# A four-layer graph network on one core: read-outs moved between a block's scores and its products, and a new order for the end of layers two and three

## The chip, the core and the metric

The kernel runs on one core of one Trainium2 chip. The time is the device time of one execution in microseconds (us); several executions are taken and their median is given. The profile records one execution. Its times count from the start of the recorded span. Engines are called as the profile calls them: PE (matrix products), DVE (vector work), ACT (activations, copies), POOL (here it issues the gathers), SP (here it issues the plain transfers to and from memory).

## What is computed

The input is `x`, 4096 rows of 256 floats, and a 4096 x 4096 adjacency matrix `adj` that is symmetric, has ones on its diagonal and otherwise about two ones in a thousand. Four layers of attention over each row's neighbours follow one another, each with a norm before and the input added behind:

```python
h = relu(layernorm(x)); x = x + _L0(h, adj, W, a)      # 4 heads, elu
h = relu(layernorm(x)); x = x + _L1(h, adj, W, a)      # 1 head
h = relu(layernorm(x)); x = x + _L2(adj, h, w, b, phi) # 4 heads
h = relu(layernorm(x)); x = x + _L3(h, adj, Wq, ...)   # q, k, v, 4 heads

def _L1(node, adj, W, a):
    h = node @ W
    e = leaky_relu((h @ a[:F, 0])[:, None] + (h @ a[F:, 0])[None, :], 0.01)
    att = softmax(where(adj > 0, e, NEG_INF), axis=1)
    return h + att @ node

def _L2(adj, input, weights, biases, phis):
    x_prime = einsum('nd,hdf->hnf', input, weights) + biases
    S = leaky_relu(s_src[:, :, None] + s_dst[:, None, :], 0.2)
    return concat_heads(softmax(where(mask, S, -1e9)) @ x_prime)

def _L3(x, edge, Wq, bq, Wk, bk, Wv, bv):
    q, k, v = heads(x @ Wq + bq), heads(x @ Wk + bk), heads(x @ Wv + bv)
    scores = q @ k.T / sqrt(64) + (edge.T - 1) * 10000
    return merge(softmax(scores) @ v)
```

## The kernel before

The code counts layers from 0, so the layers two and three of the title are `l == 1` and `l == 2`; below, "layer 1" and "layer 2" are the code's. The rows were sorted by their number of neighbours and cut into 32 blocks of 128 rows (one row per partition). Block 0 holds the rows with most neighbours (23 slots), block 31 those with fewest (3 slots).

A first part (`lists`, `scan`) reads the adjacency matrix into lists of neighbours; `late` finishes layer 0. Then `layer(1)`, `layer(2)` and `layer(3)` run, all by the function `layer` (L1349). Each layer reads a table in memory (`tab[l]`) with one row per node, and layers 1 and 2 write the table of the next one: while layer `l` runs over its blocks, the rows of layer `l+1` are made from the blocks that are finished.

`layer` is a loop of 32 steps over the blocks in the order `ORDER` = 0, 30, 1, 29, ... 14, 16, 15, 31: it alternates large and small blocks, and ends with 14, 16, 15, 31. In a step these parts come, each for the block that it is due for:

- `fill` (L1368): POOL issues one indirect gather per neighbour slot (`fetch`, L1048), up to `AHEAD` = 4 steps ahead, into a ring in on-chip memory. The first gather of a layer waits until all rows of its table are in memory.
- `scores` (L1538): for layer 2 DVE adds the two score parts (L1553, L1554), the leaky slope (L1565), the maximum (L1596) and subtracts it (L1597); ACT takes the exponential (L1600). For layer 1 ACT adds (L1550, L1551), DVE compares neighbour lists (L1608, L1612), takes slope and maximum (L1565, L1592), and ACT the exponential (L1594).
- `weigh` (L1615): DVE sums and inverts (L1626, L1627), scales the shares (L1628), the row's own part (L1639) and the gathered rows (L1654, up to eight slots at a time, two at a time in the last two blocks); PE adds all slots up in PSUM by products with the identity (L1634, L1662), and a last product (L1668) ends the block.
- `settle` (L1675): DVE sums the two halves of PSUM into `x` (L1689) and takes the norm's statistics (L960, L962). The first half of `normed` is ACT's chain of eight small instructions (L965 to L972).
- `norm`: ACT makes `h` (L975), PE transposes it (L985, two instructions). `flip`: ACT copies the transpose out of PSUM as `ht` (L987).
- `product`: the first part of `advance` (L1695): PE multiplies `ht` with the next layer's weights (L1028). In layer 1 that is one product of width 264 (`we_l`); in layer 2 a product `wkv` of width 512 and a product `w_q` of width 256, which shares a PSUM bank with the next transposes where it can.
- `third`: the second part of `advance`. In layer 1 the row is copied out of PSUM by ACT (L1710), or for the last two blocks of ORDER by DVE with the bias added (L1708), and SP sends it to memory (L1712). In layer 2 DVE adds the bias to k and v into a tile `kv` (L1728), SP sends it (L1730), DVE adds the bias to q (L1732), multiplies q with k (L1735), reduces that per head into `eself` (L1739), and ACT takes the sums of squares of q and of k (L1742, two instructions with a read of the accumulator each).

`advance`, `settle` and `turned` are generators: each part of them runs where the loop calls `next`. Names: "norm 31" is the norm of block 31, "sum 16" the L1689 of block 16, "kv13" the L1728 of block 13, "ht14" the L987 of block 14, "squares 19" the two L1742 of block 19.

The order in which each engine executes is the order in which the code issues: an engine takes its instructions one after another, and one that waits holds up those behind it on the same engine. `upto(name, k)` runs a part for all blocks of ORDER up to place `k`. The loop sets how many steps each part trails: the sum by `S` (2, or 1 in the last five steps), the norm by `N` (3, then 2), the row's product by `Q` (5, 4, 3, 2 towards the end), its read-out by `T = Q + 1`.

Four PSUM banks are lent and given back by name (`bank`, `give`), so a product can wait for the read-out of an earlier one. The tiles `kv` come from a pool with three buffers (L1727): the L1728 of a block overwrites the tile of the block three earlier, once everything that reads that tile is done. The row's read-outs wait for the last product of an earlier step (`told_by`, `signals`) in place of their own product where that stands behind it on PE. At the end of layer 2 a check of the bounds (`verdict`, L1758) reads the squares.

The core of the old order in `layer`, cut:

```python
upto("norm", i - N); upto("product", i - Q)
p = self.scores(l, b, self.rows[b], g)
sums[b] = self.weigh(l, b, ..., g, p)
upto("settle", i - S); upto("flip", i - F); upto("third", i - T)
```

Of the kernel before, what the change touches and what calls it, by code (L numbers as in the profile page):

```python
# [20 lines left out]
D = 256  # L21
# [34 lines left out]
ORDER = [0, 30] + [b for k in range(1, 15) for b in (k, 30 - k)] + [15, 31]  # L56
# [24 lines left out]
class Sparse:  # L81
# [365 lines left out]
    def constants(self):  # L447
# [5 lines left out]
        for k, by in enumerate((MARK + PAIR, MARK)):  # L453
# [217 lines left out]
    def sort(self):  # L671
# [677 lines left out]
    def layer(self, l):  # L1349


        nc, nt, vs = self.nc, self.nt, {}
        wide = (W, WL, W, 2 * D)[l]
        slots = RING // wide
        ring = self.ring[:, : slots * wide].rearrange("p (k w) -> p k w", w=wide)
        todo, held, at = list(ORDER), {}, 0
# [67 lines left out]
        sums, behind, turning, flipped, rows = {}, {}, {}, {}, {}  # L1424
# [49 lines left out]
        def third(d):  # L1474
            if l < 3:
                step, wrote = when["row", d]
                self.reads = []
                next(rows.pop(d), None)
                if step < now:
                    for i in self.reads:  # L1480
                        told_by(i, wrote, step)
            while made and (len(made) > 1 or todo == []):
                i = self.send(*made.pop(0)).ins
                next_in_line(i)
                self.tc.declare_no_dep(i, group="results", reason="places differ")
                self.tc.add_to_no_dep_group("results", i)

        stages = {"settle": settle, "norm": norm, "flip": flip, "product": product, "third": third}
        done = {name: 0 for name in stages}

        def upto(name, k):
            while done[name] <= k:
                stages[name](ORDER[done[name]])
                done[name] += 1

        for i in range(nt):
            now = i
            left = nt - 1 - i
            if l == 3:
                S = 1 if left < 3 else 2  # L1500
                N = F = Q = S + 1
                T = N
            else:
                S = 1 if left < 5 else 2
                N = 2 if left < 4 else 3
                Q = 2 if left < 2 else 3 if left < 4 else 4 if left < 6 else 5
                F, T = max(N, Q - 1), Q + 1
            fill(i)
            if (l, i) == (2, 4):
                self.symmetric()  # L1510
            b = ORDER[i]
            upto("norm", i - N)
            upto("product", i - Q)
            g = ring[:, held[b][0] : held[b][1], :]
            p = self.scores(l, b, self.rows[b], g)
            if l == 3:
                upto("third", i - T)
            sums[b] = self.weigh(l, b, vs.pop(b) if l == 3 else self.rows[b][:, 0:D], g, p)
            start, end = held.pop(b)
            past.append((start * wide, end * wide, self.read))  # L1520
            self.ever.append((start * wide, end * wide, self.read[0]))
            if l < 3:
                signals[i] = self.read[1]
            upto("settle", i - S)
            if l < 3:
                upto("flip", i - F)
                upto("third", i - T)
        now = nt
        upto("norm", nt - 2)
        upto("third", nt - 3)  # L1530
        upto("product", nt - 2)
        upto("settle", nt - 1)
        upto("norm", nt - 1)
        upto("third", nt - 2)
        upto("product", nt - 1)
        upto("third", nt - 1)

    def scores(self, l, b, mine, g):  # L1538

        nc, pool = self.nc, self.pool  # L1540
        H = 1 if l == 1 else 4
        G = self.slots(l, b)
        K = CAPS[b]
        more = b == 0
        e = pool.tile([P, TOPK, H], F32, name=f"s_e_{l}_{b}", tag="e", bufs=3)
        ek = e[:, : K + 1, :].rearrange("p k h -> p (k h)")
        if l < 3:
            src = mine[:, D + H : D + 2 * H]
            if l == 1:
                nc.scalar.activation(e[:, :G, 0], g[:, :G, D], AF.Identity, bias=src)  # L1550
                nc.scalar.activation(e[:, K, :], mine[:, D : D + H], AF.Identity, bias=src)  # L1551
            else:
                first = nc.vector.tensor_tensor(e[:, K, :], mine[:, D : D + H], src, ALU.add)  # L1553
# [11 lines left out]
            steep = nc.vector.scalar_tensor_tensor(ek, ek, slope, ek, ALU.mult, ALU.max)  # L1565
# [34 lines left out]
        nc.scalar.activation(p[:, : K + 1, :].rearrange("p k h -> p (k h)"), ek, AF.Exp)  # L1600
        return p, p, None
# [13 lines left out]
    def weigh(self, l, b, me, g, made):  # L1615
# [6 lines left out]
        exps, p, tot = made  # L1622
# [20 lines left out]
        if more:  # L1643
            rows = self.more_rows(l, p, g[:, KEPT, :])
# [50 lines left out]
    def advance(self, l, b, ht, made):  # L1695
# [5 lines left out]
        if l == 2:  # L1701
# [5 lines left out]
            if short:  # L1707
                i = nc.vector.tensor_tensor(mine, ps, self.be2, ALU.add)  # L1708
            else:
                i = nc.scalar.copy(mine, ps)  # L1710
            self.reads.append(i.ins)
            nc.sync.dma_start(out=self.tab[2][ts(b, P), :], in_=mine)  # L1712
        else:
# [14 lines left out]
            i = nc.vector.tensor_tensor(kv, ps, self.bqkv[:, D:], ALU.add)  # L1728
# [52 lines left out]
class Net:  # L1781
# [341 lines left out]
    def dot_attention(self, wq, bq, wk, bk, wv, bv):  # L2123
        nc, tc, nt, n, nb = self.nc, self.tc, self.nt, self.n, self.nb
        scale = 1.0 / 8.0
        with ExitStack() as ctx:
# [88 lines left out]
            for b in range(nb):  # L2215
# [45 lines left out]
                while waiting:  # L2261
                    weigh()
# [58 lines left out]
```

## Time and profile before

| what | us |
|---|---|
| runs shown | 1676.06, 1674.33, 1669.05; median 1674.33 |
| the profiled execution | 1670.3 |
| its span, first to last instruction | 1668.5 |
| busy in the span: POOL, DVE, PE, ACT | 1142.3, 1108.8, 1074.4, 536.1 |

Cut at the first and last gathers of the layers, the same execution divides as follows (busy time of the engines in each stretch):

| stretch | us | PE | DVE | ACT | POOL |
|---|---|---|---|---|---|
| lists of neighbours | 0 to 375 | 248.8 | 271.2 | 204.4 | 229.1 |
| rest of layer 0 | 375 to 545 | 109.9 | 120.7 | 67.9 | 117.7 |
| layer 1, gathers | 545 to 875.9 | 232.5 | 163.0 | 110.4 | 250.2 |
| its end, no gathers | 875.9 to 902.7 | 16.4 | 10.6 | 10.7 | 0.95 |
| layer 2, gathers | 902.7 to 1240.2 | 238.8 | 215.1 | 104.5 | 255.6 |
| its end, no gathers | 1240.2 to 1275.2 | 25.5 | 22.3 | 16.1 | 0.95 |
| layer 3 | 1275.2 to 1668.5 | 202.5 | 305.9 | 22.3 | 287.8 |

In the lists of instructions by time, a line gives the start, the busy time, the engine, the source line, the operation with its output and inputs, the shape, and in brackets how long the engine had been idle before and what ended that; no bracket means that the engine went straight on. In the lines by stretches, each engine has its busy time and its number of instructions, and `PEclk` is the granted clock of PE as a share of full speed.

### The profile page before, as it was taken

How to read it: one execution, taken by the hardware profiler on the slowest of the kernel's cores; microseconds unless marked ns; L12 is line 12 of the kernel's file. 1: busy time of each engine (PE TensorE's matmuls, PEld its weight loads, DVE VectorE, ACT ScalarE, POOL GpSimd, SP SyncE). 2: the span in 40 equal slices, each digit the busy share in tenths (PEclk: the TensorE clock that was granted, in tenths of full speed). 3: DMA queues.
4: the chain of work that ended last, by engine and by line, in shares of the span. 5: the costliest groups of instructions: out<-in, count | busy, mean ns of one | idle time of the engine just before them, and what ended most of it. 6: DMA issues, size and time to landing. Idle time of an engine off the chain costs nothing.

```text
span 1668.5 us, 14028 instructions
## 1 busy us (share of the span) xinstructions
PE 1074.4 (64%) x3166; PEld 583.3 (35%) x3179; DVE 1108.8 (66%) x2651; ACT 536.1 (32%) x1754; POOL 1142.3 (68%) x1241
## 2 busy tenths in 40 slices
PE   5858888605775367787773567777793455546465
PEld 4513333203443234444442234444352232323232
DVE  5669899816885255555552456777774897888786
ACT  6966664103354033343342023333342000000000
POOL 1267777767774777777772777777753777777775
PEclk9969899857898678788897689999997677877777
DMA  7899999466552444444452445444543777767674
GB/s 267 298 395 394 365 394 331 147 222 162 155 166 69 119 120 127 132 131 134 131 137 65 108 111 148 133 139 133 142 123 106 210 220 205 213 206 211 201 209 132
DMA packets 125908, 309.07 MB, mean 185 GB/s; under 512 B 35028, under 2 KB 53463, under 8 KB 125816
## 3 DMA queue, kind: packets, MB, share of 16 engines
q0 software_dynamic: 66832, 203.64, 42.5%
q1 hardware_dynamic: 58984, 104.46, 17.8%
q8 instruction: 27, 0.44, 0.1%
q14 instruction: 65, 0.53, 0.1%
HBM read 273.00 MB, written 35.00 MB: 185 GB/s over the span
## 4 chain that ended last, share of the span: by engine, by line
POOL 25%; DVE 22%; DMA 20%; issue 15%; ACT 8%; PE 8%; DVEq 0%; POOLq 0%; ACTq 0%; SPq 0%
POOL s_ring L1048 20%; DMA s_ring<-s_tab,s_near 12%; DMA s_raw<-in_adj_dram 6%; DVE s_ring L1654 5%; POOL s_g L1048 2%; DMA s_g<-s_tab,s_keep 2%; POOL s_placed L722 2%; DVE s_ring L1575 1%; ACT s_low L277 1%; PE s_acc L1272 1%; PE s_acc L1662 1%; PE s_bank L1028 1%; DVE s_e L1579 1%; PE s_ps_t L1028 1%; POOL out_dram L1065 1%
## 5 line engine op out<-in xcount | busy, mean ns | idle before, releaser
L1048 POOL DMA_INDIRECT s_ring<-s_tab,s_near x900 | 855.9, 951 | 338.0 <-issue 264.8
L1662 PE MATMUL s_acc<-s_ring,s_ident 128*128 128x512 f32 (+1 forms) x1002 | 459.8, 616 | 275.6 <-DVE s_ring L1654 275.1
L1662 PEld LDWEIGHTS s_acc<-s_ring,s_ident 128*128 128x128 f32 x1002 | 222.2, 229 | 489.7 <-DVE s_ring L1654 305.2
L1048 POOL DMA_INDIRECT s_g<-s_tab,s_keep x192 | 182.8, 952 | 128.5 <-DMA s_raw<-in_adj_dram 66.1
L1654 DVE TENSOR_TENSOR s_ring<-s_ring,s_shares 128x2048 f32<-128x2048 f32 (+1 forms) x153 | 232.9, 1552 | 0.0
L277 ACT ACTIVATE s_low<-s_raw 128x1024 fp8e4<-128x1024 int32 x128 | 135.0, 1055 | 58.6 <-DMA s_raw<-in_adj_dram 56.8
L1600 ACT ACTIVATE s_shares<-s_e 128x40 f32<-128x40 f32 (+7 forms) x64 | 13.1, 205 | 332.7 <-DVE s_e L1597 332.7
L520 PE MATMUL s_pt<-s_low,s_mark_True 128*128 128x512 fp8e4 x256 | 83.9, 408 | 53.2 <-DVE s_cand L532 46.6
L1575 DVE TENSOR_TENSOR s_ring<-s_ring,s_shares 128x2048 f32<-128x2048 f32 (+7 forms) x47 | 78.8, 1676 | 56.4 <-DMA s_ring<-s_tab,s_near 36.4
L965 ACT ACTIVATE s_y<-s_mv,s_eps 128x1 f32<-128x1 f32 x64 | 18.8, 294 | 276.4 <-DVE s_mv L962 250.4
L532 DVE MAX8 s_cand<-s_pt 128x8 f32<-128x256 f32 x256 | 93.1, 416 | 13.8 <-PE s_pt L530 12.3
L1608 DVE TENSOR_SCALAR s_eq<-s_ring,s_own_f 128x207 bf16<-128x207 f32 (+12 forms) x32 | 12.6, 393 | 134.0 <-DMA s_ring<-s_tab,s_near 133.6
L631 PE MATMUL s_ae<-s_g,s_ident 128*128 128x512 f32 x192 | 93.0, 614 | 3.0 <-DVE s_g L622 2.9
L1579 DVE TENSOR_REDUCE s_e<-s_ring 128x32 f32<-128x2048 f32 (+7 forms) x47 | 78.9, 1679 | 1.6
L1028 PE MATMUL s_bank<-s_wkv,s_ht 128*128 128x512 f32 x128 | 63.6, 621 | 3.5 <-ACT s_ht L987 3.5
L520 PEld LDWEIGHTS <-s_mark_True 128*128 128x128 bf16 x256 | 23.6, 101 | 104.8 <-issue 61.1
L1634 PE MATMUL s_acc<-s_rx,s_ident 128*128 128x256 f32 x192 | 59.3, 392 | 0.0
L1028 PE MATMUL s_ps<-s_we_l,s_ht 128*128 128x264 f32 x128 | 43.7, 493 | 23.5 <-ACT s_ht L1310 23.5
L1668 PE MATMUL s_acc<-s_me,s_ident 128*128 128x256 f32 x192 | 57.6, 382 | 0.0
L1307 PE MATMUL s_pht<-s_ident,s_rx 128*128 128x128 f32 x64 | 14.0, 323 | 66.0 <-DMA s_ring<-s_tab,s_near 49.3
L622 DVE TENSOR_TENSOR s_g<-s_g,s_pe 128x1536 f32<-128x1536 f32 x32 | 55.4, 1735 | 0.0
L924 PE MATMUL s_bank<-s_to,s_to_row 128*128 128x32 f32 (+1 forms) x6 | 1.8, 393 | 81.8 <-DVE s_to L918 81.8
(286 smaller groups left out, 1830.8 us busy)
## 6 DMA issues: line engine op xcount, KB each, us to landing
s_raw<-in_adj_dram SPq DMA_DIRECT2D x128, 512.0 KB, 9.6
s_ring<-s_tab,s_near POOLq DMA_INDIRECT x900, 2.9
s_rx<-s_placed SPq DMA_DIRECT2D x32, 262.0 KB, 3.3
s_tab<-s_kv SPq DMA_DIRECT2D x32, 256.0 KB, 2.3
s_tab<-s_rx SPq DMA_DIRECT2D x32, 132.0 KB, 1.9
s_keep<-in_x_dram SPq DMA_DIRECT2D x8, 512.0 KB, 7.5
s_vself<-s_tab SPq DMA_DIRECT2D x32, 128.0 KB, 3.5
s_tab<-s_keep SPq DMA_DIRECT2D x7, 528.0 KB, 3.7
```

The costliest lines, as they stand in the source:

```text
L277: nc.scalar.activation(low[r][:, quarter(q)], raw.pop(q), AF.Copy, saturate=False, accum_out=self.sums[:, r, h : h + 1],)
L520: nc.tensor.matmul(pt, lhsT=self.mark[k], rhs=lo[:, k * PAIR + g * IB : k * PAIR + (g + 1) * IB], start=(k == 0), stop=False,)
L532: nc.vector.max(out=cand[:, g * (IB // CH) + k, :], in_=pt[:, ts(k, CH)])
L631: self.behind(got, nc.tensor.matmul(acc, lhsT=self.ident, rhs=g[:, :, k, 0:D], start=False, stop=(k == E - 1)))
L1028: self.writes(self.nc.tensor.matmul(ps[:, :width], lhsT=ht[:, c, :], rhs=w[:, c, :], start=(c == 0 and bias is None), stop=(c == KC - 1),))
L1048: return self.nc.gpsimd.indirect_dma_start(out=out, out_offset=None, in_=table[:, :], in_offset=bass.IndirectOffsetOnAxis(ap=idx, axis=0),)
L1575: scaled = nc.vector.tensor_tensor(kq, kq, q.unsqueeze(1).to_broadcast([P, m, D]), ALU.mult)
L1579: nc.vector.tensor_reduce(e[:, k0 : k0 + m, :], kq.rearrange("p k (h d) -> p k h d", h=4), AX.X, ALU.add)
L1634: self.took_x[b] = nc.tensor.matmul(acc[:, 1, :], lhsT=self.ident, rhs=self.x[b], start=True, stop=False)
L1654: scaled = nc.vector.tensor_tensor(v, v, p[:, k0 : k0 + m, :].unsqueeze(3).to_broadcast([P, m, H, D // H]), ALU.mult)
L1662: self.behind(self.got.get((l, b), ()), nc.tensor.matmul(acc[:, 0:n, :], lhsT=self.ident, rhs=g[:, k : k + n, v0 : v0 + D], start=False, s ...
L1668: last = nc.tensor.matmul(acc[:, 0, :], lhsT=self.ident, rhs=mev, start=False, stop=True).ins
```

## The change

The parts stay the same; the loop that orders them is written anew, and the second part of `advance` is cut in two in layer 2.

- Layers 1 and 2, all but the last two steps: `third` (the row's read-out and its transfer) runs between a step's `scores` and its `weigh`, where it ran behind the step's `settle` and `flip`.
- The last two steps of both layers: the last block's scores are issued directly behind the last but one block's products and norm; sum 16 goes ahead of block 15's products, and sum 15 ahead of block 31's.
- Layer 2: q times k, its reduction and the two squares become a part `rest` of their own. With more than four steps left it runs right behind `third`. After that it is left until `third` is about to run for the block three later (`upto("rest", done["third"] - 3)`), and at the end for all that remain. The kv pool keeps its three buffers.
- `self.turns`, which picks one of two buffers for the shares, is counted on in `scores` in place of `weigh`, as two blocks' scores can now be open.
- Layer 3 keeps its order.

```diff
-                next(rows.pop(d), None)
+                upto("rest", done["third"] - 3)
+                next(rows[d], None)
...
+        def rest(d):
+            next(rows.pop(d), None)
...
-        for i in range(nt):
-            now = i
-            left = nt - 1 - i
...
-            upto("norm", i - N)
-            upto("product", i - Q)
-            g = ring[:, held[b][0] : held[b][1], :]
-            p = self.scores(l, b, self.rows[b], g)
-            if l == 3:
-                upto("third", i - T)
-            sums[b] = self.weigh(l, b, vs.pop(b) if l == 3 else self.rows[b][:, 0:D], g, p)
...
-            upto("settle", i - S)
-            if l < 3:
-                upto("flip", i - F)
-                upto("third", i - T)
-        now = nt
-        upto("norm", nt - 2)
-        upto("third", nt - 3)
-        upto("product", nt - 2)
-        upto("settle", nt - 1)
-        upto("norm", nt - 1)
-        upto("third", nt - 2)
-        upto("product", nt - 1)
-        upto("third", nt - 1)
+        def score(i):
+            b = ORDER[i]
+            if i not in scored:
+                scored[i] = self.scores(l, b, self.rows[b], block(i))
+
+        def weigh(i):
...
+            sums[b] = self.weigh(l, b, me, block(i), scored.pop(i))
...
+        def shape(i):
+            upto("norm", i)
+            upto("flip", i)
+            upto("product", i)
+
+        for i in range(nt):
+            left = nt - 1 - i
...
+            elif left > 1:
+                S = 1 if left < 5 else 2
+                N = 2 if left < 4 else 3
+                Q = 3 if left < 4 else 4 if left < 6 else 5
+                upto("norm", i - N)
+                upto("product", i - Q)
+                score(i)
+                upto("third", i - Q - 1)
+                if left > 4:
+                    upto("rest", i - Q - 1)
+                weigh(i)
+                upto("settle", i - S)
+                upto("flip", i - max(N, Q - 1))
+            elif left == 1:
+                upto("norm", i - 2)
+                upto("product", i - 2)
+                score(i)
+                upto("settle", i - 1)
+                upto("third", i - 3)
+                weigh(i)
+                upto("norm", i - 1)
+                score(i + 1)
+            else:
+                shape(i - 2)
+                upto("third", i - 3)
+                upto("settle", i - 1)
+                weigh(i)
+                upto("third", i - 2)
+                shape(i - 1)
+                upto("settle", i)
+                upto("norm", i)
+                upto("third", i - 1)
+                shape(i)
+                upto("third", i)
+                upto("rest", i)
...
         p = self.shares[:, ts(self.turns % 2, TOPK * H)].rearrange("p (k h) -> p k h", h=H)
+        self.turns += 1
...
-        self.turns += 1
...
             self.reads.append(i.ins)
+            yield
             qk = pool.tile([P, 4, 64], F32, name=f"s_qk_{b}", tag="qk", bufs=2)
```

More of the change, by code (lines that the diff above doesn't have):

```diff
@@ L1486, in third @@
                 self.tc.add_to_no_dep_group("results", i)
-        stages = {"settle": settle, "norm": norm, "flip": flip, "product": product, "third": third}
+        def rest(d):
+            next(rows.pop(d), None)
+        stages = {
+            "settle": settle, "norm": norm, "flip": flip, "product": product, "third": third,
+            "rest": rest,
+        }
         done = {name: 0 for name in stages}
@@ L1494, in upto @@
                 done[name] += 1
-        for i in range(nt):
-            now = i
-            left = nt - 1 - i
-            if l == 3:
[L1500 to L1510, printed above, removed]
-            b = ORDER[i]
-            upto("norm", i - N)
-            upto("product", i - Q)
-            g = ring[:, held[b][0] : held[b][1], :]
-            p = self.scores(l, b, self.rows[b], g)
-            if l == 3:
-                upto("third", i - T)
-            sums[b] = self.weigh(l, b, vs.pop(b) if l == 3 else self.rows[b][:, 0:D], g, p)
+        block = lambda i: ring[:, held[ORDER[i]][0] : held[ORDER[i]][1], :]
+        scored = {}
+        now = 0
+        def score(i):
+            b = ORDER[i]
+            if i not in scored:
+                scored[i] = self.scores(l, b, self.rows[b], block(i))
+        def weigh(i):
+            nonlocal now
+            b = ORDER[i]
+            me = vs.pop(b) if l == 3 else self.rows[b][:, 0:D]
+            sums[b] = self.weigh(l, b, me, block(i), scored.pop(i))
             start, end = held.pop(b)
@@ L1522, in layer @@
             if l < 3:
-                signals[i] = self.read[1]
-            upto("settle", i - S)
-            if l < 3:
-                upto("flip", i - F)
-                upto("third", i - T)
-        now = nt
-        upto("norm", nt - 2)
-        upto("third", nt - 3)
-        upto("product", nt - 2)
-        upto("settle", nt - 1)
-        upto("norm", nt - 1)
-        upto("third", nt - 2)
-        upto("product", nt - 1)
-        upto("third", nt - 1)
+                signals[i], now = self.read[1], i + 1
+        def shape(i):
[4 more added lines that the diff above has]
+            left = nt - 1 - i
+            fill(i)
+            if (l, i) == (2, 4):
+                self.symmetric()
+            if l == 3:
+                S = 1 if left < 3 else 2
+                score(i)
+                upto("third", i - S - 1)
+                weigh(i)
[11 more added lines that the diff above has]
+                weigh(i)
+                upto("settle", i - S)
+                upto("flip", i - max(N, Q - 1))
+            elif left == 1:
+                upto("norm", i - 2)
+                upto("product", i - 2)
+                score(i)
+                upto("settle", i - 1)
[7 more added lines that the diff above has]
+                upto("settle", i - 1)
+                weigh(i)
+                upto("third", i - 2)
[6 more added lines that the diff above has]
+                upto("rest", i)
+        if l == 3:
+            upto("third", nt - 3)
+            upto("settle", nt - 1)
+            upto("third", nt - 1)
     def scores(self, l, b, mine, g):
```

## The prediction

> **What bounds the kernel now.** I read the granted clock and span first, then busy time by stretches, then the gathers on POOL, then the two tails on each engine in order of time.
>
> ```profile
> core 0: us, PE busy (x) PEld busy (x) DVE busy (x) ACT busy (x) POOL busy (x), PEclk, DMA share, GB/s
> 850.00:876.00 26.00, 19.76 (x68) 11.02 (x66) 12.57 (x28) 13.95 (x57) 19.60 (x22) 1.00 0.53 138
> 876.00:902.70 26.70, 16.33 (x56) 10.22 (x56) 10.59 (x30) 10.57 (x44) 0.89 (x2) 0.86 0.14 45
> 1215.00:1241.00 26.00, 24.74 (x82) 14.35 (x80) 21.28 (x51) 13.73 (x58) 19.91 (x21) 1.00 0.53 146
> 1241.00:1275.20 34.20, 25.07 (x77) 13.76 (x77) 21.98 (x59) 15.36 (x60) 0.17 (x1) 0.95 0.15 54
> ```
> ```profile
> 1240.23 0.95 POOL L1048 DMA_INDIRECT s_ring<-s_tab,s_near  x1 [0.30 <-issue]
> 1275.22 0.94 POOL L1048 DMA_INDIRECT s_ring<-s_tab,s_near  x1 [34.05 <-PE s_bank L1767]
> ```
>
> POOL issues a gather every 1.25 us (0.95 busy, 0.30 of issue) and stops only where a layer ends: 875.93 to 902.69 (26.8) and 1240.23 to 1275.22 (35.0). The next layer's first gather needs every row in memory, so a tail lasts until block 31's row has landed. The releaser named, L1767, is not it: block 31's L1728 ran at 1271.66 and its DMA was issued at 1272.38, 2.8 us before the gather. Elsewhere only POOL's rate counts. The note for later: ahead of tail one DVE is busy 12.57 of 26.0, ahead of tail two 21.28, so there is little cover there.
>
> **Steady steps.** The two programs' instruction orders show POOL and SP unchanged, and on DVE, ACT and PE the same instructions in another order. In code layer 1 one ACT copy (L1710, 0.36) goes ahead of the norm chain; in layer 2 four DVE operations (L1728, L1732, L1735, L1739: starts 0.58, 0.44, 0.46 and 0.46 apart, 1.9 us) go from behind the step's sums to between its scores and L1626, and four square instructions (L1742) move with them on ACT. I cost this at nothing over some 54 steps, since the gathers hide it; were that cover gone, 1.9 us a step is the price. Layer 3 keeps its order: nothing. SP's row DMA is issued by the row's read-out, so it moves with it.
>
> **Tail one (layer 1).**
>
> ```profile
> 885.88 0.16 DVE L1565 SCALAR_TENSOR_TENSOR s_e<-s_e 128x4 f32<-128x4 f32 x1 [3.79 <-ACT s_e L1551]
> 888.42 0.68 DVE L1689 TENSOR_REDUCE s_rx<-s_acc 128x256 f32<-128x512 f32 x1
> 890.26 0.69 DVE L1689 TENSOR_REDUCE s_rx<-s_acc 128x256 f32<-128x512 f32 x1 [0.47 <-PE s_acc L1668]
> 893.00 0.37 ACT L987 COPY s_ht<-s_bank 128x256 f32<-128x256 f32 x1 [0.26 <-PE s_bank L985]
> 893.26 0.30 ACT L965 ACTIVATE s_y<-s_mv,s_eps 128x1 f32<-128x1 f32 x1
> ```
>
> Block 31's scores wait 3.79 for ACT, which is at block 16's norm; block 15's sum then starts at 888.42 though its last product ended at 883.11; and block 31's norm starts at 893.26 behind ht15, though its statistics were ready at 891.63. Changed: sum 16 and its statistics (1.3 us: starts 880.25 to 881.42, plus 0.1) go ahead of block 15's products; the first PE product there is held by PE (879.08), so they start some 0.3 later and the last ends at 883.45. Sum 15 at 883.5, its statistics end at 884.85; L1627 of 31 there; to its first product 0.74 (886.75 to 887.49), then 2.72 to the end of L1668 (887.49 to 890.21): 888.3. ACT's row copy of 16 waits for that (0.26), h15 to ht15 takes 1.13 (891.87 to 893.00), ht15 0.26: norm 31 at 889.95 instead of 893.26. The 9.43 from there to the gather stays. **Gain 3.3.** Were sum 16's 1.3 us to lie wholly on the path, 2.2.
>
> **Tail two (layer 2).**
>
> ```profile
> 1240.70 0.69 DVE L1728 TENSOR_TENSOR s_kv<-s_bank,s_bqkv 128x512 f32<-128x512 f32 x1 [1.13 <-PE s_acc L1668]
> 1244.47 0.37 ACT L987 COPY s_ht<-s_bank 128x256 f32<-128x256 f32 x1 [3.11 <-PE s_bank L1028]
> 1246.13 0.15 DVE L1553 TENSOR_TENSOR s_e<-s_rx 128x4 f32<-128x4 f32 x1
> 1255.74 0.17 DVE L1626 TENSOR_REDUCE s_t<-s_shares 128x4 f32<-128x16 f32 x1 [2.80 <-ACT s_shares L1600]
> 1262.40 0.69 DVE L1728 TENSOR_TENSOR s_kv<-s_bank,s_bqkv 128x512 f32<-128x512 f32 x1 [1.58 <-PE s_acc L1668]
> 1264.25 0.68 DVE L1689 TENSOR_REDUCE s_rx<-s_acc 128x256 f32<-128x512 f32 x1
> 1265.65 0.29 ACT L965 ACTIVATE s_y<-s_mv,s_eps 128x1 f32<-128x1 f32 x1 [0.82 <-DVE s_mv L962]
> ```
>
> The tail's two waits, 2.80 and the 1.85 by which sum 31 stands behind kv16's four operations, are what the change goes at. But with four steps left, q times k and the squares now trail by up to three blocks, and the kv pool still has three buffers: L1728 of a block waits for the squares of the block three earlier (13 for 19, 14 for 18, 16 for 13, 15 for 17), issued on ACT just before. Where before it waited for PE alone, DVE now queues behind ACT's whole queue.
>
> Step 16 (before: statistics of 17 done 1229.62, first product 1234.19). After, kv18 stands ahead of the product. Squares 11 are done 3.45 behind the statistics (norm 1.79, h 0.49, exp 0.22, squares 0.94), while DVE is there after 1.9 (scores 0.95, q×k and reduce 0.92): a 1.6 wait. Then L1728 and L1732 1.02, L1626 to L1639 1.02: first product at +5.6 instead of +4.57. Step 14 adds a wait of the same kind, now for PE's row product in front of the block's own products: I take 2.4 late at the start of step 16 (bounds 0 and 2.9, a whole step's wait and read-out). Together 3.5 to 3.9 late: first product of 16 at 1237.9.
>
> From there:
> - Block 16's last product: 6.46 behind the first (1234.19 to 1240.65): 1244.4. ACT: ht17 0.25, h14 0.6, transposes 0.4; PE row 17 2.75 (1241.69 to 1244.44), since ht14 shares a bank with it (the 3.11 wait above): ht14 at 1248.6; squares 19 0.94: 1249.85. DVE had come to kv13 at 1242.4, so it **stands for 7.5 us**; kv13 was at 1240.70 before.
> - kv13 1.02, q×k 0.92, kv17 1.02, then scores 15 at 1252.8 (before 1246.13), done 1253.9; sum 16 and statistics 1.3; L1626 to L1639 1.0; products 1256.4 to 1258.9; scores 31 1.0; q×k 0.92: 1260.8.
> - kv14 waits for squares 18 behind ht16: L1668 of 15 ends 4.9 behind the first product (1248.41 to 1253.28): 1261.3, transposes 0.4, ht16 0.25, squares 0.94: 1262.95, 2.1 of waiting. kv14 1.02, sum 15 1.3, L1626 of 31 1265.3, products to 1267.3, q×k 0.92, kv16 behind squares 13 at 1269.1, done 1270.1; sum 31 with statistics 1271.4.
> - Norm 31 at 1271.55 instead of 1265.65. The 9.57 from there to the gather keeps its make-up (squares between h31 and ht31 as before). **Loss 5.9.** With nothing late at step 16 but its own 1.0, it is 3.5; with 2.9 from step 14, 6.4.
>
> **Sum.** 1668.5 − 3.3 + 5.9 = 1671.1 of span, +2.6. The profiled execution took 1670.3, 1.8 around its span, 4.0 under the median of 1674.33. On the median: **1676.9**. Own range, by the bounds: −3.3 + 3.5 to −2.2 + 6.4, 1674.5 to 1678.5; with the scatter of the runs shown (1669.05 to 1676.06) some 1671 to 1682.
>
> [...] In 1257 to 1260 the granted clock was 0.50 and row 16's wkv product took 2.72 instead of 1.88, though PE had paused only 0.97, 1.48 and 0.46 us just before. [...]
>
> **Rivals.**
> 1. *Tail two gains as well.* If the squares are on ACT early enough that no L1728 waits, the two old waits go: −2.80 − 1.85 − 3.3 = −7.9: 1666.4. For it: ACT is busy only 15.36 of 34.2 in the tail. Against: ACT's idleness is waiting in order (3.11 for PE, before ht14), and squares 19 stand behind exactly that. Chance 0.12.
> 2. *Slower by PE's clock.* Place: tail two from 1244 on. Each row pair at half clock costs 1.6 to 1.7 (2.72 + 1.91 against 1.98 + 1.03) and a block's ten products up to 3.7 more. The path crosses the products of 16, row 17, the products of 15, and row 31. With the products of 15 and two row pairs slow: 3.7 + 3.3 = 7.0 on top: 1683.9. It decides once two pairs and one block of products are slow: 8.4 over before is 5.8 over my sum. For it: the 0.50 rows, and longer pauses. Against: 0.95 over the old tail as a whole. Chance 0.25.
> 3. *It does nothing that counts:* both tails keep within 1 us, since the last row is late anyhow: 1674. For: outside the tails POOL alone sets the pace. Against: the chains above. Chance 0.15.
>
> My forecast has the rest, 0.48. A measurement of this kernel tells about 0.5% (8.4 us) from no change: faster is below 1666.0, slower above 1682.7. Rival 1 lies at the edge (0.10 faster), rival 2 mostly beyond, with a little of mine: 0.27; same 0.63. The range 1667 to 1686 leaves out about 0.2.
>
> **What would show it.** Right: the first stop of POOL some 23.5 long, the second near 41; L1728 of block 13 late by about 9 us and released by ACT L1742; norm 31 of layer 1 directly behind ht15. Wrong: L1728 released by PE as before, a second stop under 35, or a gather stream in layer 2 with stops of its own, which would put the 1.9 us a step on the path. A clock near 0.5 in the second stop is rival 2.

## The result: slower by 0.4%, and where the time went

| | before | changed |
|---|---|---|
| median of 18 runs each, us | 1673.39 | 1679.35 |
| range of the runs | 1668.92 to 1678.08 | 1675.94 to 1685.23 |
| ratio, 95% interval | | 1.0038 [1.0027, 1.0048] |

That is 6.0 us, with 4.5 to 8.0 in the interval: inside the forecast range of 1667 to 1686 and on the forecast side, but more than twice the 2.6 that was worked out, and above the 0.2 to 4.2 to which the sum's own bounds came. By the prediction's own 0.5% it counts as "same", yet with 18 runs each the interval excludes no change.

The stops of POOL in the profile of the changed kernel (span 1683.5; its execution was the longest of the 18), from the gathers in order of time, first around the end of layer 1, then of layer 2:

```profile
881.88 0.95 POOL L1048 DMA_INDIRECT s_ring<-s_tab,s_near  x1 [0.30 <-issue]
907.50 0.95 POOL L1048 DMA_INDIRECT s_ring<-s_tab,s_near  x1 [24.66 <-issue]
...
1246.27 0.95 POOL L1048 DMA_INDIRECT s_ring<-s_tab,s_near  x1 [0.30 <-issue]
1290.25 0.95 POOL L1048 DMA_INDIRECT s_ring<-s_tab,s_near  x1 [43.03 <-DVE s_nm L1804]
```

From start to start, 25.6 us for the first stop and 44.0 for the second. With the starts of the gathers every execution can be cut into the same stretches; a stop runs from the layer's last gather to the next layer's first:

| us | start of layer 1 | gathers 1 | end of layer 1 | gathers 2 | end of layer 2 | layer 3 |
|---|---|---|---|---|---|---|
| before | 539.5 | 336.4 | 26.8 | 337.5 | 35.0 | 393.3 |
| changed | 544.7 | 337.2 | 25.6 | 338.8 | 44.0 | 393.2 |
| difference | +5.2 | +0.8 | −1.2 | +1.3 | +9.0 | −0.1 |

The 5.2 lie in code that is the same in both, so they are scatter of these two executions; the stretches that the change touches make 9.9, where the medians show 6.0. So the table gives places, not sizes to the microsecond: the profiled execution of the kernel before was 3.1 under its median, that of the changed kernel 5.9 over. The end of layer 1 is shorter in this pair, though by less than forecast, and the end of layer 2 is 9 us longer.

The end of layer 2 on its engines in order of time, as the prediction showed it for the kernel before (L1769 is now the kv read-out, L1784 the squares, L1709 a block's last product, L1594 the first instruction of the scores, L1695 the products on DVE):

```profile
1245.52 0.69 DVE L1769 TENSOR_TENSOR s_kv<-s_bank,s_bqkv 128x512 f32<-128x512 f32 x1 [1.74 <-ACT s_sq L1784]
1247.47 2.28 DVE L1695 TENSOR_TENSOR s_ring<-s_ring,s_shares 128x2048 f32<-128x2048 f32 x1
1257.96 0.37 ACT L987 COPY s_ht<-s_bank 128x256 f32<-128x256 f32 x1 [3.11 <-PE s_bank L1028]
1259.31 0.69 DVE L1769 TENSOR_TENSOR s_kv<-s_bank,s_bqkv 128x512 f32<-128x512 f32 x1 [7.52 <-ACT s_sq L1784]
1261.97 0.15 DVE L1594 TENSOR_TENSOR s_e<-s_rx 128x4 f32<-128x4 f32 x1
1271.62 0.69 DVE L1769 TENSOR_TENSOR s_kv<-s_bank,s_bqkv 128x512 f32<-128x512 f32 x1 [2.43 <-ACT s_sq L1784]
1277.60 0.69 DVE L1769 TENSOR_TENSOR s_kv<-s_bank,s_bqkv 128x512 f32<-128x512 f32 x1 [1.02 <-ACT s_e L1612]
1279.93 0.29 ACT L965 ACTIVATE s_y<-s_mv,s_eps 128x1 f32<-128x1 f32 x1 [1.60 <-DVE s_mv L962]
1283.70 2.89 PE L1028 MATMUL s_bank<-s_wkv,s_ht 128*128 128x512 f32 x4 [0.76 <-ACT s_ht L987]
```

The 7.52 before kv13 is the stand that the prediction put at 7.5: DVE waits for ACT, whose ht14 waits 3.11 for PE's row product, as before the change, while the squares that free the tile stand behind it. kv14 waits 2.43 (forecast 2.1), kv16 1.02. Block 31's norm starts at 1279.93, 33.7 us after the last gather; before it was 25.4.

A view of what DVE's L1769 (before L1728) and its second half wait for while layer 2's gathers run, after and before (total us, times, longest):

```profile
DVE s_kv L1769 <- PE s_acc L1709: 35.4, 12, 6.0
DVE s_kv L1769 <- PE s_bank L1028: 3.1, 2, 2.1
DVE s_kv L1769 <- ACT s_sq L1784: 1.7, 1, 1.7
```
```profile
DVE s_rx L1732 <- ACT s_ht L987: 33.4, 22, 1.6
DVE s_kv L1728 <- PE s_acc L1668: 2.7, 2, 1.5
DVE s_kv L1728 <- PE s_bank L1028: 0.6, 1, 0.6
```

The sums are alike, some 40 and 37 us, but not their place. Before, they came when the block's products were already on PE; now DVE waits up to 6.0 us for the last block's final product, and the products that PE could do next stand behind that wait on DVE. The gathers hide it in the steady steps; near the end of the layer nothing does.

What DVE waits for there is not the row product that the read-out reads. By `told_by` a read-out waits for the last product of the step in which its row product was issued. Behind the next block's products, where the read-outs stood before, that wait was mostly over; ahead of them it holds up DVE. The read-out of block 10, PE and DVE in order of time:

```profile
1195.30 1.03 PE L1028 MATMUL s_bank<-s_w_q,s_ht 128*128 128x256 f32 x4
1199.97 6.75 PE L1703 MATMUL s_acc<-s_ring,s_ident 128*128 128x256 f32 x10 [3.21 <-DVE s_ring L1695]
1206.56 0.59 PE L1709 MATMUL s_acc<-s_me,s_ident 128*128 128x256 f32 x2
1207.19 0.69 DVE L1769 TENSOR_TENSOR s_kv<-s_bank,s_bqkv 128x512 f32<-128x512 f32 x1 [6.00 <-PE s_acc L1709]
```

Block 10's own products had ended at 1196.33, before this wait began. A version in which the moved read-outs wait for their own products was not run.

### The profile page after: what moved, and what is told of

The parts are those of the page before. It is cut to its first block, busy times and chain, and to the rows that moved or that the text cites. A ratio compares the mean times of both kernels' runs of the same rounds, so it can differ in the third digit from the quotient of the medians.

```text
span 1683.5 us, 14012 instructions
## 1 busy us (share of the span) xinstructions
PE 1081.3 (64%) x3166; PEld 589.1 (35%) x3179; DVE 1104.9 (66%) x2651; ACT 536.9 (32%) x1754; POOL 1145.7 (68%) x1241
## 4 chain that ended last, share of the span: by engine, by line
POOL 30%; DMA 20%; issue 19%; DVE 17%; PE 8%; ACT 6%; DVEq 0%; POOLq 0%; ACTq 0%; SPq 0%
POOL s_ring L1048 25%; DMA s_raw<-in_adj_dram 9%; DMA s_ring<-s_tab,s_near 8%; DVE s_ring L1695 4%; PE s_acc L1703 4%; ACT s_low L277 2%; POOL s_placed L722 2%; POOL s_g L1048 2%; PE s_ps_t L1028 1%; DVE s_ring L1616 1%; POOL out_dram L1065 1%; PE s_bank L1028 1%; DVE s_e L1620 1%; DVE s_ring L1264 1%; PE s_acc L1272 1%
## 5 line engine op out<-in xcount | busy, mean ns | idle before, releaser
L1703 PE MATMUL s_acc<-s_ring,s_ident 128*128 128x512 f32 (+1 forms) x1002 | 464.9, 622 | 311.1 <-DVE s_ring L1695 311.1
L1695 DVE TENSOR_TENSOR s_ring<-s_ring,s_shares 128x2048 f32<-128x2048 f32 (+1 forms) x153 | 233.0, 1554 | 0.0
L1769 DVE TENSOR_TENSOR s_kv<-s_bank,s_bqkv 128x512 f32<-128x512 f32 x32 | 22.0, 688 | 55.4 <-PE s_acc L1709 35.4
L1709 PE MATMUL s_acc<-s_me,s_ident 128*128 128x256 f32 x192 | 57.4, 381 | 0.0
L1595 DVE TENSOR_TENSOR s_e<-s_ring,s_rx 128x36 f32<-128x36 f32 (+12 forms) x32 | 6.2, 193 | 77.6 <-DMA s_ring<-s_tab,s_near 66.6
```

What stands on the lines that cost most here:

```text
L1695: scaled = nc.vector.tensor_tensor(v, v, p[:, k0 : k0 + m, :].unsqueeze(3).to_broadcast([P, m, H, D // H]), ALU.mult)
L1703: self.behind(self.got.get((l, b), ()), nc.tensor.matmul(acc[:, 0:n, :], lhsT=self.ident, rhs=g[:, k : k + n, v0 : v0 + D], start=False, s ...
L1709: last = nc.tensor.matmul(acc[:, 0, :], lhsT=self.ident, rhs=mev, start=False, stop=True).ins
```

## Experiments

Two theories stood against each other for the loss at the end of layer 2. A: the three kv buffers and the deferred squares make DVE wait for ACT. B: the read-outs ahead of the products make DVE wait for PE. The changed kernel itself was run only in the comparison above.

The runs met three chips. On two of them PE issued in some stretches only one instruction every 1.40 us, mostly without anything that the profile shows it waiting for, and the kernel before itself took 1978 to 1997 us; on the third it took 1674.8. So a ratio is always to the kernel before on the same chip, and the stretches are compared within a group only. An example of such a stretch, PE in order of time with the new order in layer 1 alone (L1728 is there the slots' product):

```profile
1149.77 0.59 PE L1728 MATMUL s_acc<-s_ring,s_ident 128*128 128x256 f32 x1 [2.21 <-issue]
1152.57 0.58 PE L1728 MATMUL s_acc<-s_ring,s_ident 128*128 128x256 f32 x1 [2.21 <-DMA s_ring<-s_tab,s_near]
1155.37 1.01 PE L1728 MATMUL s_acc<-s_ring,s_ident 128*128 128x512 f32 x1 [2.21 <-issue]
1158.17 1.01 PE L1728 MATMUL s_acc<-s_ring,s_ident 128*128 128x512 f32 x1 [1.78 <-issue]
```

A product and its weight load, two instructions, come every 2.80 us. Intervals of 1.38 to 1.42 us between the starts of neighbouring PE instructions (products and weight loads) occur 67 to 95 times in each of the eleven traces of those two chips, and 4 times each in the trace before, the changed kernel's and the one of the third chip.

**Four kv buffers** (e1_kv4, e5_kv4_again, e9_kv4_third: one kernel). The room comes from a second q-times-k tile and from layer 3's output tiles:

```diff
-            tag = ("out", "kv")[ORDER.index(b) % 2]
+            tag = ("out", "kv", "kv")[ORDER.index(b) % 3]
-            ... tag=tag, bufs=3)[:, 0:D]
+            ... tag=tag, bufs={"out": 2, "kv": 4}[tag])[:, 0:D]
-            kv = pool.tile([P, 2 * D], F32, name=f"s_kv_{b}", tag="kv", bufs=3)
+            kv = pool.tile([P, 2 * D], F32, name=f"s_kv_{b}", tag="kv", bufs=4)
-            qk = pool.tile(..., tag="qk", bufs=2)
+            qk = pool.tile(..., tag="qk", bufs=1)
```

> Changed kernel with four kv buffers instead of three (a second q-times-k tile is given up for the room, and layer 3 alternates its output tiles otherwise), so L1769 of a block waits for the squares of the block four earlier. Theory A (the cost is DVE standing behind ACT's queue for the kv buffer): in the changed kernel's profile the waits of L1769 for ACT are 1.74 (kv18), 7.52 (kv13), 2.43 (kv14), 1.02 (kv16) and 2.76 us (kv15). With block 11's squares done at 1245.5, kv13 could go at 1251.7 and kv17 at about 1257.1, where PE's row 17 ends, so scores 15 come about 3.8 us earlier; 2.4 and 1.0 follow. The end of layer 2 should fall from 44.0 to about 36 to 38 us, and the time from 1679.4 to 1671 to 1673. Theory B (the cost is the read-out itself ahead of the products: DVE waits for PE's previous block there, so PE idles and its clock falls): the end of layer 2 stays over 41 us and the time within 2 us of 1679.4.

> The kernel of e1_kv4 again, as the first four runs met a chip on which the kernel before itself took 1996.8 us. Theory A (DVE stands behind ACT's queue for the kv buffer): no L1769 near the end of layer 2 waits for an L1784 over 1 us, the end of layer 2 is 36 to 38 us instead of 44.0, and the time is 1671 to 1673 where the kernel before takes 1673.4 (ratio 0.998 to 1.000). Theory B (the read-out ahead of the products is what costs, as DVE waits for PE's previous block there and PE idles): over 41 us, ratio 1.002 to 1.004.

> The kernel with four kv buffers once more: on the two chips so far PE issued in some stretches only one instruction every 0.70 or 1.40 us, and the kernel before took 1978 and 1997 us there. On a chip where the kernel before takes about 1673: Theory A (DVE stands behind ACT's queue for the kv buffer) gives an end of layer 2 of 36 to 38 us instead of 44.0 and a ratio of 0.998 to 1.000; Theory B (the read-out ahead of the products makes DVE wait for PE) gives over 41 us and 1.002 to 1.004. If PE is held back again: as on the two chips before, ratio 1.010 to 1.016, end of layer 2 10 us or more over that of e7_layer1_again (84.1).

Measured: 1.0106 [1.0062, 1.0151] and 1.0154 [1.0115, 1.0192] on the two chips that hold PE back. On the third chip 1675.37 against 1674.79, 1.0005 [0.9995, 1.0014]: below the changed kernel's interval and at the kernel before, though 1.0005 lies between what the two theories named. The end of layer 2 was 41.0 us there, which is neither A's 36 to 38 nor B's "over 41". The stop of POOL, and the waits in order of time (first in the last steps with gathers, then at the end):

```profile
1232.37 0.69 DVE L1769 TENSOR_TENSOR s_kv<-s_bank,s_bqkv 128x512 f32<-128x512 f32 x1 [3.01 <-PE s_bank L1028]
...
1250.89 0.69 DVE L1769 TENSOR_TENSOR s_kv<-s_bank,s_bqkv 128x512 f32<-128x512 f32 x1 [2.24 <-PE s_acc L1709]
1254.81 0.37 ACT L987 COPY s_ht<-s_bank 128x256 f32<-128x256 f32 x1 [3.11 <-PE s_bank L1028]
1256.17 0.69 DVE L1769 TENSOR_TENSOR s_kv<-s_bank,s_bqkv 128x512 f32<-128x512 f32 x1 [3.47 <-ACT s_sq L1784]
...
1284.60 0.94 POOL L1048 DMA_INDIRECT s_ring<-s_tab,s_near  x1 [40.01 <-DVE s_qk L1777]
```

The 7.52 of kv13 are gone; it waits 2.24 for PE. But with four buffers kv17 takes the tile of block 19, whose squares stand behind the same ht14: 3.47. Half of the stand has moved one block on: kv13 starts 7.2 us after the last gather instead of 13.0, kv17 only 12.5 instead of 14.8, and the end is 3.0 us shorter. So A is real.

Its size shows on more than one chip in the last stretch of the layer, from the end of block 17's statistics (L962) to the next layer's first gather. With three buffers and the new order it takes 48.4 us in the changed kernel's trace and 48.8 in e4_layer2_only, where kv13 stands for the same 7.52; with four buffers it takes 45.3 in each of three traces on three chips; before the change it took 45.5. That is some 3 of the 9 us. The other 6 are there before this stretch begins: block 17's statistics end 4.4 us ahead of the last gather in the changed kernel and 4.3 with four buffers, but 10.5 ahead before the change. The fourth buffer does not touch them.

The two ratios, each taken on its own chip, differ by 0.0033, some 5.5 us of 1674. Three of them are this wait; 1.3 may come from the other output tiles, as layer 3 took 391.9 instead of 393.2 in the traces; the rest is open. And the medians of the third chip leave only 0.6 us between four buffers and before (at most 2.3), so the 6 us of lateness in these single traces cannot be what executions pay on average, unless something else gains as much.

**Squares at once** (e2_rest_now, e6_rest_now_again): q times k and the squares directly behind every read-out, in the last steps too, three buffers.

```diff
-                upto("rest", done["third"] - 3)
                 next(rows[d], None)
...
+                upto("rest", done["third"])
```

> Changed kernel with q times k, its reduction and the squares directly behind every read-out again, three kv buffers; the read-outs stay ahead of the products and the last steps keep their new order. Theory A: the squares are then on ACT three blocks ahead of the next user of the tile, no L1769 waits for an L1784 over 0.5 us, and the end of layer 2 is 36 to 39 us (1.84 us of DVE work per block, four blocks, go back into the tail; some 7 us of waits go): 1672 to 1675. Theory B: over 41 us, 1677 to 1681.

> The kernel of e2_rest_now again. Theory A: no L1769 waits for an L1784 over 0.5 us, the end of layer 2 is 36 to 39 us, ratio to the kernel before 0.999 to 1.001. Theory B: over 41 us, ratio 1.002 to 1.005.

Measured: 1.0161 [1.0121, 1.02] and 1.0203 [1.017, 1.0237], with ends of layer 2 of 101.8 and 96.6 us. No L1766 (the kv read-out there) near the end waits for the squares any more, as A said, and the last stretch from block 17's statistics on takes 46.9 us in both. The time is not better for it: on the first of the two chips layer 2 alone with the deferral has 1.0155 (below). From the changed kernel it differs only in the last steps, where two more DVE operations stand ahead of a block's products. On the third chip it wasn't run.

**The new order in one layer alone** (e3_layer1_only, e7_layer1_again, e10_layer1_third; e4_layer2_only). In the other layer the old loop stands as it was (for e4_layer2_only the same with `l == 1`):

```diff
+            elif l == 2:
...
+                upto("norm", i - N)
+                upto("product", i - Q)
+                score(i)
+                weigh(i)
...
+                upto("settle", i - S)
+                upto("flip", i - max(N, Q - 1))
+                upto("third", i - Q - 1)
...
```

> New order in layer 1 alone; layer 2 keeps the order of the kernel before. Theory A (the loss is all in layer 2; layer 1 gains 1.1 as in the changed kernel's profile, up to the 3.3 of the prediction): end of layer 1 23.5 to 25.7 us instead of 26.8, end of layer 2 35 us, time 1670 to 1672 against 1673.4 before. Theory B (what was moved costs in the steady steps of both layers as well): the time is above 1674.

> The kernel of e3_layer1_only again. Theory A: end of layer 1 23.5 to 25.7 us instead of 26.8, end of layer 2 35 us, ratio 0.998 to 0.9995. Theory B: ratio above 1.0005.

> New order in layer 1 alone, on a chip where the kernel before takes about 1674 (if it is such a one). Theory A (layer 1 gains, all the loss is in layer 2): end of layer 1 23.5 to 26 us instead of 26.8, gathers of layer 2 337 to 338 us, end of layer 2 35 us, ratio 0.998 to 0.9995. Theory B (the moved read-outs cost in layer 1 too, so that the new end only makes up for it): 1.000 or more.

> New order in layer 2 alone; layer 1 keeps the order of the kernel before. Theory A: end of layer 1 26.8 us, end of layer 2 43 to 44 us, time 1680 to 1683, that is 1 to 3 over the changed kernel. If the end of layer 2 is nearer to the prediction's 40.9 than to the 44.0 of the one profile, the half clock in that profile (block 14's products in layer 1 took 7.21 us instead of 4.14) was of that execution: then 1678 to 1680.

Measured: layer 1 alone 1.0007 [0.9975, 1.0038], 1.0028 [0.9996, 1.006] and 0.9979 [0.9946, 1.0012]; layer 2 alone 1.0155 [1.0111, 1.0199]. Layer 1's part is not to be told from nothing in three tries, and all of the loss that these chips show sits in layer 2. The layer 1 runs all met chips that hold PE back; whether the part gains its 1 us on the third chip stays open.

**Four buffers and the read-outs back behind the products** (e8_kv4_behind, e11_kv4_behind), and **the new last two steps alone** (e12_ends_only: read-outs behind, squares at once, three buffers):

```diff
                 score(i)
-                upto("third", i - Q - 1)
-                if left > 4:
-                    upto("rest", i - Q - 1)
                 weigh(i)
                 upto("settle", i - S)
                 upto("flip", i - max(N, Q - 1))
+                upto("third", i - Q - 1)
+                if left > 4:
+                    upto("rest", i - Q - 1)
```

> As e5_kv4_again (four kv buffers), and the read-outs of both layers are put back behind the step's products, sums and flip; the deferral of q times k and the new order of the last two steps stay. Theory A: the place of the read-outs does not matter as long as no L1769 waits for squares: end of layer 2 within 1.5 us of e5_kv4_again's, ratio within 0.001 of it. Theory B: 3 us or more shorter than in e5_kv4_again, 32 to 34 us, ratio 0.995 to 0.998.

> Four kv buffers, and the read-outs of both layers behind the step's products, sums and flip again; the deferral and the new order of the last two steps stay. With four buffers alone the end of layer 2 was 41.0 us, and L1769 still waited 1.15 to 3.01 us for PE in the steps before it, ahead of the block's own products. Theory B (those waits are the rest of the loss): end of layer 2 34 to 37 us, ratio 0.996 to 0.999. Theory A' (what is left comes from the squares that still stop L1769 of block 17 for 3.47 us, and from the deferred work in the tail): 39 to 41 us, ratio 0.9995 to 1.001.

> The kernel before with only the new order of the last two steps in layers 1 and 2 (last scores behind the last but one's products, sum 16 ahead of block 15's products, sum 15 ahead of block 31's); read-outs behind the flips, q times k and squares directly behind them, three kv buffers. If the two waits of the old tail (2.80 us of L1626 of block 31 for ACT, 1.85 us of sum 31 behind kv16) can be had without the other two parts: end of layer 2 31 to 34 us, end of layer 1 24 to 26 us, ratio 0.996 to 0.9985, the best of all versions. If the new end itself moves the wait on (sum 16 and sum 15 now stand ahead of products): 35 us or more, ratio 0.9995 to 1.001.

Measured: 1.0077 [1.0045, 1.011] and 1.0019 [0.9987, 1.005]; the ends alone 1.0041 [1.0006, 1.0075]. All three ran where PE is held back. The stretches of every trace of those chips, sorted by where layer 2's read-outs stand (us):

| kernel | read-outs of layer 2 | gathers 2 | end of layer 2 | from block 17's statistics on |
|---|---|---|---|---|
| layer 1 alone (3 traces) | behind, old end | 378.3, 378.6, 381.0 | 84.1, 85.9, 87.5 | 44.3, 46.9, 46.9 |
| four buffers, behind (2) | behind, new end | 377.3, 378.5 | 92.4, 88.0 | 50.6, 52.4 |
| ends alone (1) | behind, new end | 378.6 | 94.7 | 54.1 |
| four buffers (2) | ahead, new end | 392.4, 394.3 | 98.5, 96.7 | 45.3, 45.3 |
| squares at once (2) | ahead, new end | 393.2, 394.8 | 101.8, 96.6 | 46.9, 46.9 |
| layer 2 alone (1) | ahead, new end | 395.3 | 102.4 | 48.8 |

Layer 2's gathers take 377.3 to 381.0 us wherever the read-outs stand behind the products and 392.4 to 395.3 wherever they stand ahead: 11.4 to 16.5 us within a group, with no overlap, whatever the buffers, the deferral and the end. The cleanest pair is e5_kv4_again and e8_kv4_behind, four buffers on one chip, where the place of the read-outs is the only difference: 394.3 against 378.5 us, and medians of 2004.6 against 1991.3. That is B, where PE is slow enough that the gathers no longer cover it. On the third chip the gathers take 338.6 with four buffers, against 337.5 before: there the cover holds.

The whole end of layer 2 is 8.7 us longer with the read-outs ahead in that pair. In the last stretch it is the other way round: 50.6 to 54.1 us with the read-outs behind and the new end, 45.3 to 48.8 with them ahead. In all three of those traces a read-out right behind block 17's statistics waits 4.70, 6.40 and 5.47 us for PE's last product, where before the change it waited for nothing. The new loop counts the step on in `weigh`, so `told_by` there makes a read-out behind the products wait for the last product of its own step. So these three kernels are not the old order with one part exchanged, and the new last two steps were never tried by themselves without that wait.

How much of the 6 us of lateness B makes on an undisturbed chip was not run by itself; the waits of L1769 for PE in the traces above are what speaks for it, and PE's clock, below, is mixed in.

No version tried is shown to beat the kernel before. Four buffers get the changed kernel level with it.

## Why the prediction was right in its direction and too small

- **The steady steps: costed at nothing.** Nearly so on an undisturbed chip: +0.8 and +1.3 us over the two layers. The condition was named (the gathers hide it, and 1.9 us a step is the price without them); where PE is held back, some 15 us over layer 2 is what it became.
- **Tail two, the wait on the kv buffer: right.** kv13 stood for 7.52 us (forecast 7.5), released by L1784, behind an ht14 that waited 3.11; kv14 waited 2.43 (forecast 2.1). With a fourth buffer the wait at kv13 went and the last stretch became 3.1 us shorter.
- **Tail two, the size: the step that failed is "I take 2.4 late at the start of step 16 (bounds 0 and 2.9, a whole step's wait and read-out)".** Statistics of 17 were done 4.4 us before the last gather; before the change, 10.5: 6.1 late. The prediction took one step's wait, for PE's row product. The trace has five in a row, in the steps of 13, 17 and 14: kv read-outs that waited 6.00, 0.92, 3.49, 1.70 and 2.14 for PE, and lateness that is not made up adds. The 6.00, 3.49 and 1.70 are not for a row product but for the last product of the block before, by `told_by`. Part of that is PE's clock: block 18's ten products, for which the 6.00 are, took 6.75 us at a granted clock of 0.54, where block 16's ten took 3.71 at 1.00. How the 6.1 divide between the waits' place and the clock stays open. kv13 was so 3.4 later than forecast, norm 31 2.3 (from there to the gather, with PE's row 31 at a granted clock of 0.62, it then took 0.75 more): 44.0 in place of 40.9.
- **Tail one: the step that failed is "they start some 0.3 later".** Block 15's first DVE product started 5.4 us after the last gather, and 1.9 before: 3.4 later. From there the forecast chain held: sum 16 ahead, sum 15 at 892.15 straight behind its last product, norm 31 directly behind ht15 (lines below), so the gain came out at 1.2 instead of 3.3. What was late is PE and a new wait for it: block 14's products, two blocks earlier, took 7.21 us instead of 4.14 (granted clock 0.57 instead of 1.00), and ht17, which stands ahead of block 15's scores on ACT, waits 2.29 for the last of the products behind them, those of block 16. Its own transposes were done at 876.68, and before the change it waited for these alone and ran without a stand: the new loop counts the step on in `weigh`, ahead of the flip, so `told_by` takes that step's last product. The prediction had no term for this wait.

Block 14's products in layer 1, PE in order of time, before, after, and with four buffers (layer 1 is there the same as after):

```profile
862.21 4.14 PE L1662 MATMUL s_acc<-s_ring,s_ident 128*128 128x256 f32 x12 [2.68 <-DVE s_ring L1654]
```
```profile
868.82 7.21 PE L1703 MATMUL s_acc<-s_ring,s_ident 128*128 128x256 f32 x12 [2.68 <-DVE s_ring L1695]
```
```profile
866.36 6.92 PE L1703 MATMUL s_acc<-s_ring,s_ident 128*128 128x256 f32 x12 [0.75 <-DVE s_ring L1695]
```

And the end of layer 1 after the change (ACT and DVE in order of time, behind ht17's transposes on PE):

```profile
876.30 0.38 PE L985 MATMUL s_bank<-s_ident,s_h 128*128 128x128 f32 x2
882.74 0.37 ACT L987 COPY s_ht<-s_bank 128x256 f32<-128x256 f32 x1 [2.29 <-PE s_acc L1709]
885.25 0.68 DVE L1730 TENSOR_REDUCE s_rx<-s_acc 128x256 f32<-128x512 f32 x1
887.24 2.47 DVE L1695 TENSOR_TENSOR s_ring<-s_ring,s_shares 128x512 f32<-128x512 f32 x4
892.15 0.69 DVE L1730 TENSOR_REDUCE s_rx<-s_acc 128x256 f32<-128x512 f32 x1 [1.72 <-PE s_acc L1709]
898.32 0.37 ACT L987 COPY s_ht<-s_bank 128x256 f32<-128x256 f32 x1 [0.53 <-PE s_bank L985]
898.58 0.30 ACT L965 ACTIVATE s_y<-s_mv,s_eps 128x1 f32<-128x1 f32 x1
```

- **Rival 1 (tail two gains as well)** fell: four L1769 of the end waited for ACT. **Rival 3 (nothing that counts)** fell too. **Rival 2 (PE's clock)** was no rival but a part: row 14 took 3.14 + 1.61 and row 31 2.89 + 1.86, both at a granted clock of 0.62, where rows 16 and 15 took 1.98 + 1.03 at 1.00, some 1.7 each, of which the path saw less, and the profile before had one such row too (16: 2.72 + 1.91 at 0.63); far from 7 more at the end, but it also reached into the steps ahead of both ends, where the prediction did not look for it.

## What to carry to other kernels

When a read is moved ahead of work that another engine lives on, ask what it waits for in the code, not only what it reads: here the reads waited for the last product of an earlier step, which had cost little behind the products. The sum of the waits stayed at some 40 us, and it was their place that cost. Before deferring the last use of a buffer, count who takes that buffer next and which queue the use then stands in: three buffers with uses three blocks behind means that the next writer waits for the whole queue of another engine (7.52 us here), and one buffer more moved half of the wait on by a block (3.47 us). And work out a tail from the state in which it is entered, adding up the lateness of several steps ahead of it, not of one.

## What the hardware showed that was not expected

PE's granted clock in the traces before and after the change is either 1.00 or 0.50; a figure between them is the mean over a stretch. In layer 1, block 14's twelve products took 4.14 us at 1.00 before and 7.21 at 0.57 after, though PE had paused 2.68 us ahead of them both times. The pause and the products, each as a stretch, after, then before (busy time of PE first, then PEld, DVE, ACT, POOL, and the clock):

```profile
866.14:868.82 2.68, 0.00 (x1) 0.00 (x0) 2.67 (x3) 0.00 (x0) 2.07 (x3) 0.89 0.54 147
868.82:876.03 7.21, 7.21 (x13) 3.83 (x14) 4.21 (x12) 3.25 (x14) 5.38 (x7) 0.57 0.42 116
```
```profile
859.53:862.21 2.68, 0.00 (x1) 0.00 (x1) 2.68 (x3) 0.00 (x0) 1.91 (x3) 1.00 0.63 187
862.21:866.35 4.14, 4.14 (x13) 2.55 (x14) 2.14 (x6) 2.42 (x10) 3.23 (x4) 1.00 0.41 109
```

So the length of that pause does not tell the two apart. What does was not shown, nor how much of it is luck of these single executions. With four buffers on the third chip the low clock lasted longer:

```profile
850.00:858.00 8.00, 4.67 (x15) 2.49 (x16) 4.03 (x7) 4.83 (x20) 6.00 (x7) 1.00 0.47 123
858.00:866.00 8.00, 7.62 (x16) 4.08 (x16) 3.79 (x8) 2.20 (x9) 6.17 (x7) 0.52 0.58 160
866.00:873.00 7.00, 6.64 (x12) 3.52 (x13) 4.00 (x13) 3.25 (x14) 5.17 (x7) 0.57 0.42 114
```

From 858 to 873 us PE was busy 14.26 of 15.00 us at 0.52 and 0.57, and it had paused only 1.59 us just before that. What held the clock down there stays open.

Two of the three chips held PE back in another way: one instruction every 1.40 us in stretches. The kernel before took 18 to 19% more time there (1978 to 1997 us against 1674.8), and on one of them the new order of layer 2, in a change that costs 0.4% elsewhere, cost 1.6% (1.0155).
